# Turning the normalised rows of a four-layer graph network by transposing transfers instead of TensorE

## The chip, the cores and the metric

The kernel runs on one core of a Trainium2 chip. A core has TensorE (PE, matrix products into PSUM), VectorE (DVE), ScalarE (ACT), GpSimd (POOL), SyncE (SP, which only issues transfers here) and 16 DMA engines that the issuing queues share. Each engine takes its instructions strictly in order and waits on semaphores. The metric is the time of one execution in device microseconds.

## The reference

`x` is 8 x 2048 x 128 in float32, `adj` a symmetric 2048 x 2048 adjacency. Four layers follow each other, each adding its result to `x`; each begins with the same normalisation:

```python
h = jnp.maximum(_layernorm(x, axis=-1), 0.0)
```

Layers 0, 1 and 3 are graph attention with rank-one scores; layer 0 in full, the others differ in scaling, a residual and the `elu`:

```python
Wh = jnp.einsum('bnc,dc->bnd', x, W)
f1 = Wh @ a1
f2 = Wh @ a2
e = jax.nn.leaky_relu(f1[:, :, None] + f2[:, None, :], negative_slope=0.2)
e = jnp.where(adj[None] > 0, e, NEG_BIG)
attention = jax.nn.softmax(e, axis=-1)
h_prime = jnp.einsum('bij,bjd->bid', attention, Wh)
return jax.nn.elu(h_prime)
```

Layer 2 is attention with four heads of 32 channels, the rows against themselves:

```python
scores = jnp.einsum('bihk,bjhk->bhij', x, x)
scores = jax.nn.leaky_relu(scores, negative_slope=ALPHA)
scores = jnp.where(adj_matrix[None, None, :, :] == 0, -jnp.inf, scores)
probs = jax.nn.softmax(scores, axis=-1)
out = jnp.einsum('bhij,bjhk->bihk', probs, x)
```

## The kernel before

The order of all instructions is written by a small planner inside the kernel, when the program is built. Every step is added with `add(engine, us, due, emit, needs, takes, frees, lag)`: the engine, an assumed duration, a due time, what it emits, the steps it needs, the buffers it takes and frees. `Plan.run` (L200 on) places steps one by one: of those that an engine could start within `WINDOW_US` of the earliest, the one with the smallest due time comes first. The resulting order of each engine is emitted as it is. So the numbers in `TOKENS`, `BEATS`, `LEADS`, `EARLY` and `SHIFTS` are due times and offsets, which only set the order; they are no measured times.

A unit is one layer of one batch. There are 32 units, 31 of which are interleaved over most of the span. Each unit first prepares its rows in four quarters of 512 rows:

- `rows_made` (L528): DVE takes statistics of `x` (L470), POOL the power (L113), ACT writes a quarter of normalised rows into an `h` tile (L537, four instructions; layer 3 adds four more, L544).
- `transposes` (L563): PE turns the quarter's four 128 x 128 blocks into a PSUM bank pair (L568).
- `Gat.beginning` (L574), layers 0, 1 and 3: ACT copies the turned quarter to `h_t` in SBUF (L589; DVE in batch 0, layer 0), PE projects it (L598), ACT takes exponentials and scales the rows into `y`.
- `Heads.beginning` (L940), layer 2: SP stores the rows to DRAM (`values`, L951); ACT writes the turned quarter, rounded, to `hi` (L963), DVE the remainder to `lo` (L967), SP stores both to DRAM (`halves`, L972), from where `s`, `m` and `v` are read back for each head (L986, L994, L999).

Then the main work follows. A token of layers 0, 1 and 3 is one DVE instruction (`front`, L766, 128 x 1024 into `zg`) and eight f32 products on PE (L775, two matmul records each). There are 768 tokens. A beat of layer 2 is two pairs of score products on PE (L1061), two exps on ACT (L1068), a mask with a sum on DVE (L1074) and the weighing products on PE (L1083). There are 512 beats; two are weighed together, in batch 7 one alone (`SINGLY`).

PSUM has eight banks. Two pairs (`pair`) serve scores, transposes, projections and the small turns alike; the rest hold sums. In SBUF there are three `h` tiles, two `h_t`, one `hi` and one `lo`, five `z`, three `zg`.

The transposes are emitted by

```python
for k in range(4):
    nc.tensor.transpose(pk[:, k, :], self.h[q][:, k, :], ident)
```

Of the kernel before, what the change touches and what calls it, by code (L numbers as in the profile page):

```python
# [8 lines left out]
F32 = mybir.dt.float32  # L9
# [3 lines left out]
U8 = mybir.dt.uint8  # L13
F8 = mybir.dt.float8e4
# [26 lines left out]
def adj_preln_d4(ctx: ExitStack, tc: tile.TileContext, x, adj, w0, a0, w1, a1, w3, a3,  # L41
# [112 lines left out]
    class Op:  # L154
# [8 lines left out]
    EARLY = dict(front=-488.9, score=652.2, exp=89.3, mask=-87.7, sums=-385.5)  # L163

    SINGLY = (7,)
# [7 lines left out]
        30: 15.0, 93: 158.9, 113: -50.7, 115: -69.2, 121: 83.4, 131: -98.9, 135: -82.4, 139: -197.1,  # L173
        143: 102.0, 147: -358.4, 151: -347.8, 1041: 215.9, 1099: -157.5, 2060: -98.7, 2063: -123.3,
        2886: -204.2, 2890: -250.3, 3168: 266.3, 3549: 134.1, 5962: 12.1, 6178: 39.8, 6183: -12.0,
    }

    class Plan:
# [4 lines left out]
        ENTER_US, LEAVE_US = 0.19, 0.13  # L183
# [16 lines left out]
        def run(self):  # L200
# [9 lines left out]
            for _ in self.ops:  # L210
# [31 lines left out]
                for name, taker in op.frees:  # L242
                    self.slots[name].append((op.end, taker if isinstance(taker, int) else taker.got[name]))
                self.order.append(op)
                for u in op.users:
                    u.left -= 1
                    u.ready = max(u.ready, op.end)
                    if not u.left:
                        ready[u.engine].append(u)

    def fast(ctx):
# [9 lines left out]
        plan = Plan(dict(pair=(4, 6), sums=(0,), more=(1,), low=0, z=5, zg=3, r=2, h=3, h_t=2, hi=1, lo=1,  # L261
# [184 lines left out]
        class Unit:  # L446
# [81 lines left out]
            def rows_made(self, part, step):  # L528
# [4 lines left out]
                def rows(op, q):  # L533
                    self.h[q] = blocks(quarter("h", bufs=3))
                    for k in range(4):
                        n = q * 4 + k
                        nc.scalar.activation(self.h[q][:, k, :], X[self.b][:, n, :], AF.Relu,  # L537
                                             scale=key["rstd"][:, n:n + 1], bias=key["nmr"][:, n:n + 1])
# [23 lines left out]

            def transposes(self, q, part, made, takes):  # L563

                def turn(op):
                    pk = ps[:, op.got["pair"], :].rearrange("p (k t) -> p k t", t=P)
                    for k in range(4):
                        nc.tensor.transpose(pk[:, k, :], self.h[q][:, k, :], ident)  # L568

                return add("PE", 0.45, self.due(part), turn, made[1:], takes=["pair"] + takes,  # L570
                           frees=[("h", made[0])])

        class Gat(Unit):
            def beginning(self):  # L574
# [6 lines left out]
                for q in range(4):  # L581
                    part = 0.2 + step * q
                    turn = self.transposes(q, part, made[q], ["h_t"])
# [3 lines left out]
                    def copy(op, q=q, turn=turn, begins=begins):  # L587
# [3 lines left out]
                    copied = add("DVE" if begins else "ACT", 0.61 if begins else 0.47, self.due(part), copy,  # L591
                                 [turn], frees=[("pair", turn)])
# [166 lines left out]
            def token(self, a, due, place, last_front, last_back, first, last, gate=None):  # L759
# [21 lines left out]
                f = add("DVE", 1.2, due - EARLY["front"], front, [last_front, r_ready, rows_in[jb], powers, gate if first else None], takes=["zg"],  # L781
# [157 lines left out]
        class Heads(Unit):  # L939
            def beginning(self):  # L940
# [13 lines left out]
                for q in range(4):  # L954
# [4 lines left out]
                    turn = self.transposes(q, part, made[q], ["hi", "lo"])  # L959

                    def high(op, q=q, turn=turn):
                        self.h_t[q, 0] = quarter("hi", F32R, 1)
                        nc.scalar.copy(self.h_t[q, 0], ps[:, turn.got["pair"], :])  # L963

                    def low(op, q=q, turn=turn):
                        self.h_t[q, 1] = quarter("lo", F32R, 1)
                        nc.vector.tensor_sub(self.h_t[q, 1], ps[:, turn.got["pair"], :],  # L967
                                             self.h_t[q, 0].bitcast(F32))
# [6 lines left out]
                    hi = add("ACT", 0.47, self.due(part), high, [turn])  # L975
                    lo = add("DVE", 0.61, self.due(part), low, [hi], frees=[("pair", turn)])
                    for k, (tag, op) in enumerate((("hi", hi), ("lo", lo))):
                        self.there.append(add("SP", 1.9, self.due(part + 0.02), lambda op, q=q, k=k: store(op, q, k),
                                              [op, kept], frees=[(tag, turn)], lag=2.5))
# [39 lines left out]
            def beats(self, heads):  # L1019
# [4 lines left out]
                for h, (start, step) in enumerate(heads):  # L1024
                    ops = self.load(h, start - 24.0)
                    for jb in range(NB):
# [3 lines left out]
                        for c2 in range(2):  # L1030
                            score = add("PE", 0.455, due - EARLY["score"] + c2, lambda op, s=s, c2=c2: self.scores(op, s, c2),
                                        [score, ops[jb // HB], ops[2]], takes=["pair"] + ["z"] * (c2 == 0))
                            if c2 == 0:
                                z_taker = score
                            exps.append(add("ACT", 1.0, due - EARLY["exp"] + c2, lambda op, s=s, c2=c2, sc=score: self.exp(
                                op, s, c2, sc.got["pair"]), [score], frees=[("pair", score)]))
# [4 lines left out]
                        mask = add("DVE", 2.3, due - EARLY["mask"], lambda op, s=s: self.mask(op, s), [mask] + exps)  # L1041
                        last.append((z_taker, mask))
                        self.masks.append(mask)
                        if jb % 2 or self.b in SINGLY:
# [3 lines left out]
                                        frees=[("z", z) for z, _ in last], tiled=True)  # L1048
# [80 lines left out]
            (1, 0, 0): (-1862.2, 4.85), (0, 1, 0): (-1216.0, 6.8), (0, 1, 1): (-220.6, 7.44),  # L1129
            (1, 0, 1): (528.7, 6.78), (2, 0, 0): (550.0, 6.16), (2, 0, 1): (-497.7, 10.12),  # L1130
            (3, 0, 0): (-82.3, 6.88), (1, 1, 0): (-1087.3, 8.75), (1, 1, 1): (-509.3, 5.83),
            (3, 0, 1): (-535.5, 4.96), (2, 1, 0): (170.9, 4.67), (2, 1, 1): (470.1, 7.94),
            (0, 3, 0): (304.0, 5.97), (0, 3, 1): (1007.2, 9.21), (3, 1, 0): (733.5, 6.81),
            (3, 1, 1): (1096.6, 5.79), (4, 0, 0): (707.7, 8.19), (4, 0, 1): (1082.3, 7.42),
            (1, 3, 0): (679.2, 7.79), (1, 3, 1): (958.8, 8.29), (4, 1, 0): (339.6, 9.68),
            (4, 1, 1): (926.2, 6.01), (5, 0, 0): (364.1, 4.11), (5, 0, 1): (713.9, 3.72),
            (2, 3, 0): (403.9, 2.85), (2, 3, 1): (779.2, 8.43), (5, 1, 0): (1329.8, 4.89),
            (5, 1, 1): (1475.1, 4.64), (6, 0, 0): (1098.2, 9.62), (6, 0, 1): (2950.0, 2.74),
            (3, 3, 0): (714.9, 6.41), (3, 3, 1): (3074.8, 6.4), (6, 1, 0): (2322.0, 7.03),
            (6, 1, 1): (4526.2, 10.07), (7, 0, 0): (2367.7, 7.52), (7, 0, 1): (2792.7, 6.45),  # L1140
            (7, 1, 0): (3548.0, 7.16), (7, 1, 1): (703.3, 8.6), (4, 3, 0): (4508.6, 7.53),
            (4, 3, 1): (5355.2, 5.92), (5, 3, 0): (4546.5, 7.89), (5, 3, 1): (5580.5, 5.75),
            (6, 3, 0): (3207.4, 5.91), (6, 3, 1): (5060.7, 8.36), (7, 3, 0): (5056.1, 5.64),
            (7, 3, 1): (6837.9, 10.03),
        }
        BEATS = {
            (0, 0): (-161.82, 3.21), (0, 1): (-919.72, 17.96), (0, 2): (-887.13, 24.2),
            (0, 3): (-199.99, 2.71), (1, 0): (-3459.48, 5.01), (1, 1): (-2558.28, 2.95),
            (1, 2): (-1489.16, 0.88), (1, 3): (-1318.69, 13.71), (2, 0): (-3871.2, 28.01),
            (2, 1): (-3418.31, 16.49), (2, 2): (-2569.33, 8.93), (2, 3): (-2119.51, 26.98),  # L1150
            (3, 0): (-1533.49, 0.19), (3, 1): (-1186.31, 15.62), (3, 2): (-748.22, 30.04),
            (3, 3): (-461.43, 41.91), (4, 0): (-305.77, 24.84), (4, 1): (-1349.31, 6.1),
            (4, 2): (13.32, 12.05), (4, 3): (19.17, 4.92), (5, 0): (-143.54, 17.7),
            (5, 1): (217.07, 37.91), (5, 2): (1547.2, 30.19), (5, 3): (2881.53, 42.93),
            (6, 0): (-65.94, 14.65), (6, 1): (985.66, 4.87), (6, 2): (1381.17, 7.9),
            (6, 3): (1254.02, 32.72), (7, 0): (-270.44, 3.58), (7, 1): (647.92, 27.69),
            (7, 2): (1457.66, 3.08), (7, 3): (2140.19, 3.89),
        }
        LEADS = {
            (0, 0): 256.75, (1, 0): 1070.77, (0, 1): 113.95, (2, 0): 1008.81, (1, 1): 1403.32,  # L1160
            (3, 0): 2680.39, (2, 1): 1534.69, (0, 3): 2009.19, (3, 1): 161.18, (4, 0): 1161.93,
            (1, 3): 732.86, (4, 1): 2419.32, (5, 0): 117.85, (2, 3): 1514.41, (5, 1): 1335.63,
            (6, 0): 823.02, (3, 3): 53.23, (6, 1): 1576.41, (7, 0): 1398.84, (4, 3): 255.55,
            (7, 1): 112.36, (5, 3): 472.39, (6, 3): 2332.33, (7, 3): 369.52, (0, 2): -172.84,
            (1, 2): 2456.2, (2, 2): 2358.43, (3, 2): -660.3, (4, 2): -1280.62, (5, 2): 1703.98,
            (6, 2): -1462.99, (7, 2): 1504.7,
# [253 lines left out]
```

## Time and profile before

| | |
|---|---|
| median of 3 runs | 2731.74 us (2730.69 to 2733.18) |
| span of the profiled execution, first to last instruction | 2729.7 us |
| L568 transposes on PE | 512 instructions, first at 10.7 us, last at 2638.8 us |
| L589 copy to `h_t` on ACT | 92, 557 to 617 ns |
| L963 `hi` on ACT, L967 `lo` on DVE | 32 each, 581 and 684 ns |
| L441 ACT over 128 x 2048 | 8, 1996 ns |
| L707 ACT copy of 128 x 1024 | 6, 1006 ns |
| L867 DVE addition of 128 x 1024 in SBUF | 6, 1219 ns |
| transfers | 196.47 MB, mean 72 GB/s |

The page gives the span of the profiled execution and no other time of its own; the median of the runs is 2.0 us above it. Busy time of an engine is the union of its instructions, and matmuls overlap, so PE's busy time includes the latency of the last of each burst. In the rows of groups the columns are line, engine, operation, tile written and read, shapes and count, then busy us, mean ns of one, and idle time of the engine just before them with what ended it. In the rows of waits: who waited for whom, us in total, times, the longest. In the rows of transfers: tiles, issuing queue, count, size of each, median us from issue to landing. In the rows of the timeline: start, us, what.

### The profile page before, as it was taken

The page shows a single profiled execution, that of the slowest core. Times are in us where ns is not written, and L with a number is a line of the kernel's source. Part 1 is how long each engine was busy: PE and PEld are TensorE (multiplying, and loading weights), DVE is VectorE, ACT ScalarE, POOL GpSimd, SP SyncE. Part 2 cuts the span into 40 slices and gives each one's busy share as a digit, 9 for nine tenths or more (in the row PEclk, how much of TensorE's full clock was granted, in tenths as well). Part 3 has the DMA queues.
Part 4 walks back from the last instruction along what each step waited for, and adds up shares of the span by engine and source line. Part 5 has one row for each costly group of instructions (what it writes and reads, how often), then busy time and mean ns, then how long its engine had stood idle before and what let it go on. Part 6 is the DMA issues. An engine that isn't in the chain of part 4 may idle for free. (4 is left out here: it accounts for less than half of the span.)

```text
span 2729.7 us, 49006 instructions
## 1 busy us (share of the span) xinstructions
PE 2621.9 (96%) x20104; PEld 2016.2 (74%) x20104; DVE 2488.5 (91%) x3304; ACT 1727.6 (63%) x2777; POOL 286.1 (10%) x143
## 2 busy tenths in 40 slices
PE   7999999999999999999999999999999899999997
PEld 6899877857766777767777777777785377666687
DVE  7767989999989999998999989999999799999987
ACT  3524465667676675666856567675655956787651
POOL 1200010111101011010101011011111101101010
PEclk9999999999999999999999999999999999999999
DMA  8003323252344233443433433424234321623211
GB/s 313 17 9 90 71 59 63 47 101 55 63 120 72 60 84 55 82 74 63 87 77 56 93 58 77 87 50 79 48 76 88 63 39 37 127 55 70 36 40 41
DMA packets 216873, 196.47 MB, mean 72 GB/s; under 512 B 142896, under 2 KB 178176, under 8 KB 210496
## 3 DMA queue, kind: packets, MB, share of 16 engines
q1 hardware_dynamic: 144112, 156.46, 22.3%
q0 software_dynamic: 72112, 36.73, 11.6%
q8 instruction: 160, 2.62, 0.4%
q14 instruction: 73, 0.60, 0.1%
q10 hardware_dynamic: 416, 0.07, 0.0%
HBM read 123.03 MB, written 33.73 MB: 57 GB/s over the span
## 5 line engine op out<-in xcount | busy, mean ns | idle before, releaser
L1068 ACT ACTIVATE z<-ps,shift 128x1024 f32<-128x1024 f32 x1024 | 1122.2, 1114 | 699.9 <-PE ps L1061 697.4
L775 PEld LDWEIGHTS ps<-y,zg 128*128 128x128 f32 x12288 | 1460.8, 192 | 74.3 <-DVE zg L766 25.4
L775 PE MATMUL ps<-y,zg 128*128 128x129 f32 x12288 | 1493.4, 276 | 16.7 <-DVE zg L766 11.9
L1074 DVE SCALAR_TENSOR_TENSOR z<-z,edge 128x2048 f32<-128x2048 f32 x512 | 1169.3, 2285 | 73.6 <-ACT z L1068 71.1
L766 DVE SCALAR_TENSOR_TENSOR zg<-r,cr,edge 128x1024 f32<-128x1024 f32 x768 | 969.0, 1277 | 92.9 <-PE ps L775 84.0
L1061 PE MATMUL ps<-m,s 128*128 128x512 f32 x2048 | 717.3, 436 | 47.3 <-ACT z L1068 44.1
L1061 PEld LDWEIGHTS ps<-m,s 128*128 128x128 f32 x2048 | 313.7, 190 | 321.9 <-ACT z L1068 222.5
L1083 PE MATMUL ps<-z,v 128*32 128x512 f32 x4096 | 502.6, 602 | 2.4 <-DVE z L1074 2.2
L1083 PEld LDWEIGHTS ps<-z,v 128*32 128x32 f32 x4096 | 103.9, 109 | 237.4 <-issue 190.5
L537 ACT ACTIVATE h<-x,nmrx,rstdx 128x128 f32<-128x128 f32 x512 | 210.6, 492 | 37.0 <-DVE nmrx L118 30.0
L113 POOL TENSOR_TENSOR rstdx<-varx,neg_half 128x16 f32<-128x16 f32 x31 | 130.1, 4196 | 568.5 <-DVE varx L108 559.4
L844 POOL DMA_DIRECT2D x<-oa x40 | 35.9, 897 | 918.0 <-DVE oa L808 269.3
L1108 POOL DMA_DIRECT2D x<-o x31 | 66.1, 2133 | 510.6 <-DVE o L1103 500.0
L598 PEld LDWEIGHTS ps<-rhs,h_t 128*128 128x128 f32 x768 | 99.3, 195 | 15.5 <-DVE h_t L589 5.1
L598 PE MATMUL ps<-rhs,h_t 128*128 128x130 f32 x768 | 104.8, 281 | 5.3 <-DVE h_t L589 4.2
L470 DVE BATCH_NORM_STATS2 st<-x 128x6 f32<-128x128 f32 x496 | 105.9, 278 | 0.7 <-DMA x<-oa 0.7
L568 PE MATMUL ps<-ident,h 128*128 128x128 f32 x512 | 80.2, 278 | 4.4 <-ACT z L1068 2.8
L568 PEld LDWEIGHTS ps<-ident,h 128*128 128x128 f32 x512 | 62.6, 142 | 21.6 <-ACT z L1068 6.1
L808 DVE TENSOR_TENSOR oa<-ps,rs 128x384 f32<-128x384 f32 x144 | 73.9, 513 | 5.0
L589 ACT COPY h_t<-ps 128x512 f32<-128x512 f32 x92 | 53.3, 582 | 37.2 <-PE ps L568 37.2
L636 ACT ACTIVATE y<-ps,y 128x128 f32<-128x128 f32 x240 | 68.4, 369 | 0.0
L814 ACT ACTIVATE oe<-oa 128x1024 f32<-128x1024 f32 x32 | 33.9, 1060 | 54.2 <-DVE oa L833 51.3
(129 smaller groups left out, 835.0 us busy)
## 6 DMA issues: line engine op xcount, KB each, us to landing
s<-halves SPq DMA_DIRECT2D x256, 128.0 KB, 2.8
m<-halves SPq DMA_DIRECT2D x64, 512.0 KB, 6.9
r<-row SPq DMA_DIRECT2D x42, 512.0 KB, 3.8
x<-oa POOLq DMA_DIRECT2D x40, 512.0 KB, 5.0
raw<-in_adj_dram SPq DMA_DIRECT2D x16, 1024.0 KB, 16.2
values<-h SPq DMA_DIRECT2D x32, 256.0 KB, 2.4
halves<-hi SPq DMA_DIRECT2D x128, 64.0 KB, 1.7
halves<-lo SPq DMA_DIRECT2D x128, 64.0 KB, 1.7
```

Of the source, the lines that this page charges most:

```text
L113: nc.gpsimd.tensor_tensor(out=rstd, in0=v, in1=neg_half, op=OP.pow)
L470: nc.vector.bn_stats(out=key["st"][:, n, :], in_=rows()[:, n, :])
L537: nc.scalar.activation(self.h[q][:, k, :], X[self.b][:, n, :], AF.Relu, scale=key["rstd"][:, n:n + 1], bias=key["nmr"][:, n:n + 1])
L568: nc.tensor.transpose(pk[:, k, :], self.h[q][:, k, :], ident)
L598: nc.tensor.matmul(pv[:, k, :C + 2], lhsT=self.h_t[q][:, k * P:(k + 1) * P], rhs=rhs, start=True, stop=True)
L766: nc.vector.scalar_tensor_tensor(z, self.r[half], self.cr[:, 0, jb:jb + 1], edge[:, jb, half * HN:(half + 1) * HN], op0=OP.max, op1=OP.mult)
L775: nc.tensor.matmul(ps[:, self.banks(half, place)[i // 3], k * CE:(k + 1) * CE], lhsT=z[:, i * P:(i + 1) * P], rhs=self.y[:, jb, :], start= ...
L808: nc.vector.tensor_mul(key["a"][:, i0:i1, :], pv[:, :, :C], r[:, i0:i1, None].to_broadcast([P, i1 - i0, C]))
L1061: nc.tensor.matmul(ps[:, lo + c, :], lhsT=self.S[h, jb // HB][:, at:at + P], rhs=self.M[h][:, (c2 * 2 + c) * 512:(c2 * 2 + c + 1) * 512], ...
L1068: nc.scalar.activation(self.z[s][:, c2 * HN:(c2 + 1) * HN], ps[:, lo:lo + 2, :].rearrange("p b t -> p (b t)"), AF.Exp, bias=shift)
L1074: nc.vector.scalar_tensor_tensor(self.z[s], self.z[s], 1.0, edge[:, jb, :], op0=OP.mult, op1=OP.mult, accum_out=self.den[:, h, jb:jb + 1])
L1083: nc.tensor.matmul(ps[c * HD:(c + 1) * HD, 0, :], lhsT=self.V[h][:, jb, :], rhs=z[:, c * 512:(c + 1) * 512], start=jb == 0, stop=jb == NB - 1,
```

## The change

In all units but batch 0, layer 0, the quarter is no longer turned by PE. `turned_by_transfer` puts three steps in its place. `split`, on ACT, copies the 512 float32 of each partition as 1024 16-bit integers into `pl`, the lower halves in one plane and the upper ones in the other. `move`, on SP, issues one transfer that transposes `pl` in 128 x 128 blocks of 16-bit elements into `tr`. `merge`, on ACT, writes the two turned planes interleaved into `h_t`, which has float32 again. Layers 0, 1 and 3 project from that `h_t`. In layer 2 ACT writes `hi` from it, DVE subtracts `hi` in place, and the transfers that store `lo` read `h_t`. In layer 2 `move` also needs the transfer that stores `values`, and the `h` tile is freed by the move; elsewhere by the split. There are two `h` tiles instead of three, one `pl`, one `tr` and no `lo`.

The planner's assumed durations are altered in several places, an operation's lag no longer counts toward a user on the same engine, and a beat's `z` may be freed before the whole weighing ends. All due times are new: `SHIFTS` are zero, `TOKENS` stand on a grid of 56 us with 3.5 us between tokens, `BEATS`, `LEADS` and `EARLY` have other values.

```diff
-    EARLY = dict(front=-488.9, score=652.2, exp=89.3, mask=-87.7, sums=-385.5)
+    EARLY = dict(front=-8.1, score=-8.25, exp=367.65, mask=-66.36, sums=-45.79)
+    PLANES, TURNED, ON_PE = 1, 1, ((0, 0),)
+    SPLIT_US, MOVE_US, MOVE_LAG_US, MERGE_US = 1.0, 1.2, 3.0, 1.0
...
-        ENTER_US, LEAVE_US = 0.19, 0.13
+        ENTER_US, LEAVE_US = 0.09, 0.21
...
-                    u.ready = max(u.ready, op.end)
+                    u.ready = max(u.ready, op.end - (op.lag if u.engine == op.engine else 0.0))
...
-        plan = Plan(dict(pair=(4, 6), sums=(0,), more=(1,), low=0, z=5, zg=3, r=2, h=3, h_t=2, hi=1, lo=1,
+        plan = Plan(dict(pair=(4, 6), sums=(0,), more=(1,), low=0, z=5, zg=3, r=2, h=2, h_t=2, pl=1, tr=1, hi=1,
...
+            def turned_by_transfer(self, q, part, made, kept=None):
+                key = {}
+                def split(op):
+                    key["pl"] = big.tile([P, 2, 4 * P], U16, tag="pl", name="pl", bufs=PLANES)
+                    nc.scalar.copy(key["pl"], self.h[q].rearrange("p k c -> p (k c)").bitcast(U16).rearrange(
+                        "p (n two) -> p two n", two=2))
+                def move(op):
+                    key["tr"] = big.tile([P, 8, P], U16, tag="tr", name="tr", bufs=TURNED)
+                    nc.sync.dma_start_transpose(out=key["tr"], in_=key["pl"].rearrange("p two n -> p (two n)"))
+                def merge(op):
+                    self.h_t[q] = quarter("h_t")
+                    nc.scalar.copy(self.h_t[q].bitcast(U16).rearrange("p (n two) -> p two n", two=2),
+                                   key["tr"].rearrange("p (two k) n -> p two (k n)", two=2))
+                parted = add("ACT", SPLIT_US, self.due(part), split, made[1:], takes=["pl"], frees=[] if kept else [("h", made[0])])
+                moved = add("SP", MOVE_US, self.due(part), move, [parted, kept], takes=["tr"],
+                            frees=[("pl", parted)] + [("h", made[0])] * (kept is not None),
+                            lag=MOVE_LAG_US)
+                return add("ACT", MERGE_US, self.due(part), merge, [moved], takes=["h_t"], frees=[("tr", moved)])
...
-                    turn = self.transposes(q, part, made[q], ["h_t"])
+                    by_pe = (self.b, layer) in ON_PE
+                    turn = self.transposes(q, part, made[q], ["h_t"]) if by_pe else None
...
+                    else:
+                        copied = turn = self.turned_by_transfer(q, part, made[q])
...
-                    turn = self.transposes(q, part, made[q], ["hi", "lo"])
+                    turn = self.turned_by_transfer(q, part, made[q], kept)
...
-                        nc.scalar.copy(self.h_t[q, 0], ps[:, turn.got["pair"], :])
+                        nc.scalar.copy(self.h_t[q, 0], self.h_t[q])
...
-                        nc.vector.tensor_sub(self.h_t[q, 1], ps[:, turn.got["pair"], :],
-                                             self.h_t[q, 0].bitcast(F32))
+                        self.h_t[q, 1] = self.h_t[q].bitcast(F32R)
+                        nc.vector.tensor_sub(self.h_t[q, 1], self.h_t[q], self.h_t[q, 0].bitcast(F32))
...
-            (1, 0, 0): (-1862.2, 4.85), (0, 1, 0): (-1216.0, 6.8), (0, 1, 1): (-220.6, 7.44),
+            (1, 0, 0): (92.0, 3.5), (0, 1, 0): (148.0, 3.5), (0, 1, 1): (204.0, 3.5), (1, 0, 1): (260.0, 3.5),
...
-            (0, 0): (-161.82, 3.21), (0, 1): (-919.72, 17.96), (0, 2): (-887.13, 24.2),
+            (0, 0): (304.8, 9.3), (0, 1): (453.55, 4.32), (0, 2): (522.61, 0.05), (0, 3): (510.06, 6.98),
...
-            (0, 0): 256.75, (1, 0): 1070.77, (0, 1): 113.95, (2, 0): 1008.81, (1, 1): 1403.32,
+            (0, 0): -228.72, (1, 0): 333.0, (0, 1): 2800.2, (2, 0): 323.39, (1, 1): 2219.45, (3, 0): 175.69,
```

## The prediction

> **What bounds the kernel now.** I read part 1 of the page first, then the busy time by stretch of the span, the groups of instructions, the waits, the timeline of single stretches and the transfers.
>
> ```profile
> PE 2621.9 (96%) x20104; PEld 2016.2 (74%) x20104; DVE 2488.5 (91%) x3304; ACT 1727.6 (63%) x2777; POOL 286.1 (10%) x143
> ```
>
> ```profile
> core 0: us, PE busy (x) PEld busy (x) DVE busy (x) ACT busy (x) POOL busy (x), PEclk, DMA share, GB/s
> 300.00:2700.00 2400.00, 2332.87 (x17646) 1742.03 (x17643) 2239.94 (x2882) 1598.75 (x2424) 249.37 (x116) 1.00 0.35 68
> 0.00:300.00 300.00, 274.07 (x2331) 259.41 (x2331) 231.97 (x406) 126.71 (x351) 36.74 (x27) 0.98 0.35 109
> ```
>
> Two engines are nearly full at once: from 300 to 2700 us PE is busy 97% and DVE 93%. ACT has a third of its time free. The granted clock is full, so no gain hides there.
>
> ```profile
> L1068 ACT ACTIVATE z<-ps,shift 128x1024 f32<-128x1024 f32 x1024 | 1122.2, 1114 | 699.9 <-PE ps L1061 697.4
> L775 PE MATMUL ps<-y,zg 128*128 128x129 f32 x12288 | 1493.4, 276 | 16.7 <-DVE zg L766 11.9
> L1074 DVE SCALAR_TENSOR_TENSOR z<-z,edge 128x2048 f32<-128x2048 f32 x512 | 1169.3, 2285 | 73.6 <-ACT z L1068 71.1
> L766 DVE SCALAR_TENSOR_TENSOR zg<-r,cr,edge 128x1024 f32<-128x1024 f32 x768 | 969.0, 1277 | 92.9 <-PE ps L775 84.0
> L568 PE MATMUL ps<-ident,h 128*128 128x128 f32 x512 | 80.2, 278 | 4.4 <-ACT z L1068 2.8
> L589 ACT COPY h_t<-ps 128x512 f32<-128x512 f32 x92 | 53.3, 582 | 37.2 <-PE ps L568 37.2
> ```
>
> A PE matmul here lasts 276 ns, but the next one starts long before that, so PE's price must be read from start to start:
>
> ```profile
> 760.68 0.60 PE L568 MATMUL ps<-ident,h 128*128 128x128 f32 x4
> 761.12 1.95 PE L775 MATMUL ps<-y,zg 128*128 128x129 f32 x16
> 762.83 0.71 PE L1061 MATMUL ps<-m,s 128*128 128x512 f32 x2
> ```
>
> The four transposes of a quarter hold PE for 0.44 us (760.68 to 761.12), a token 1.70 us; in the same way a pair of score products takes 0.54 and a beat's weighing 0.93. By such prices PE has 768 tokens, 1024 score pairs, 512 weighings and some 180 us of the rest: 2522 us, 92% of the span and hardly above DVE's 2488. PE alone doesn't bound the kernel; the two do together.
>
> ```profile
> ACT z L1068 <- PE ps L1061: 697.4, 625, 4.0
> DVE z L1074 <- ACT z L1068: 71.1, 109, 2.8
> PE ps L1061 <- ACT z L1068: 44.1, 86, 1.4
> ACT h_t L589 <- PE ps L568: 37.2, 12, 29.5
> ACT hi L963 <- PE ps L568: 22.8, 14, 7.0
> ```
>
> ACT mostly waits for PE. The last two rows are 60.0 us in which ACT stood still for the transposes that are now taken from PE.
>
> **The change part by part.**
>
> Removed from PE: the built order of the changed kernel keeps 16 of the 512 transposes, those of batch 0, layer 0, so 124 quarters go. 124 x 0.436 (the median; 0.44 above) = 54.1 us. The transposes also held one of the two PSUM pairs that scores use; PE's waits for ACT are 44 us in all, the bound of a gain there, and I count none of it. In DVE's 2488 us nothing goes: the 32 low halves now read SBUF instead of PSUM, 0.68 us each, and by half of an addition of 1024 SBUF elements (1219 ns) 0.61: 2 us, nil.
>
> The order laid out anew: I cut both built orders into stretches of 100 us of PE work and set beside each the DVE work that must be done by its end. Of one late stretch: the new order has 24 tokens and 28 beats, DVE 24 x 1.22 + 28 x 2.22 + 16 for statistics and endings = 107 us; the old one has 31 and 21 there, and 99 us. The new order puts beats later (376 of 512 by token 608, before 402), and a beat costs DVE more than PE. What DVE has beyond PE, summed over the stretches, is 39 us in the old order and 70 in the new: +32. So PE's gain is in good part lost to DVE.
>
> ACT: 92 copies of 0.58 go (-53), 124 splits and 124 joins of 1024 16-bit elements come. No row has a 16-bit copy. Bounds: 0.58 if a pair passes as one 4-byte element, 2.0 if an element two or four bytes apart costs double (L441 takes 1996 ns for 2048). I take 1.0, L707's 1006 ns for 1024 elements. 248 - 53 = +195, ACT at some 1922 us, 71%. It is hidden under the 697 us in which ACT waits for PE, except in one stretch near 2200 us, where ACT has 113 us of work beside DVE's 107: +6.
>
> The transfers: 124 on SP's queue, 0.25 MB each, 31 MB beside the page's 196 MB. From split to join ACT now waits for a landing that the trace does not show. The rows of 256 KB:
>
> ```profile
> values<-h SPq DMA_DIRECT2D x32, 256.0 KB, 2.4
> v<-values SPq DMA_DIRECT2D x32, 256.0 KB, 5.0
> x<-o POOLq DMA_DIRECT2D x31, 256.0 KB, 7.8
> ```
>
> 2.4 has pieces of 512 bytes, 5.0 pieces of 128 bytes, 7.8 pieces of 128 bytes with an addition. In the code every row of tr gathers 16-bit elements from 128 partitions, so pieces are not longer than values' 512 bytes, and v's 5.0 is nearest; 2.4 and 7.8 stay as ends. The planner's own figure, 1.2 + 3.0, is an assumption of the code and no evidence.
>
> Queued behind the waiting join are the exps, for which PE's scores wait (two PSUM pairs), and the projections of the quarter, which in PE's new order mostly stand 0 to 2 score pairs after it. What covers the landing is the ACT work between split and join: the median is 5.0 us of busy time, at 71% 7.0 us of elapsed time. For instance four rows and two exps: 4 x 0.41 + 2 x 1.10 = 3.8, elapsed 5.4. Summed over 120 quarters (the first four have nothing between), what is missing to a landing L is 11 us at L = 2.4, 32 at 4.2, 45 at 5.0, 77 at 6.0, 170 at 7.8 and 376 at 10. Against it stand the 60 us of waits for PE that go. At 5.0 the two nearly cancel; I take 0.
>
> The Trainium skill, "VectorE: DVE Perf Modes", "The three transpose paths", speaks against the change: it lists 1309 ns for a 128x128 two-byte block by DMA and 390 by TensorE, and advises TensorE where PSUM will do. Eight such blocks in a row would be 10.5 us, some 430 us missing and a time near 3085, an estimate from that page. "Advanced Engine Details and Errata", "X-Bar Transpose (TRN2)", says that such transfers are as fast as ordinary ones: then 2.4 holds, and 2678 at best. No row here decides between the pages.
>
> SP: an issue holds its queue 0.38 us by values' row; 47 us in all, under waits for scores of 950 us. But 24 of the 124 moves stand right behind loads of s or v that wait for PE (up to 38.4 us in one case before), and 16 s loads stand right behind a move, so a late split delays a load. Planned waits, priced nothing; if the cover goes, each costs what it is late. One pl and one tr tile make a unit serial: 1.0 + 5.0 + 1.0 a quarter, 28 us a unit, 868 us for 31 units; it fits in 2700. Rows held in two h tiles instead of three free up at the split or the landing: nothing while L is under the 7 us above.
>
> Sum against the span: 2729.7 - 54.1 + 32 + 6 + 0 = 2713.6. The median of the runs is 2.0 above the span: **2715.5**.
>
> **Rivals.**
> - Full gain: PE sets the end throughout, and the waits between the engines shrink with it. For it: PE's 97%. Against: DVE's 93% and the later beats. 2731.7 - 54 = 2678.
> - No change: DVE keeps its 2488 us and its 241 us of idle time, and what PE saves becomes waiting. For it: DVE zg <- PE is only 84 us in all. 2731.
> - Late transfers, slower: joins stand in ACT's queue before exps and projections. From L = 6 on (77 - 60 = 17, the whole remaining gain) the kernel is slower. At 7.8 it is 170 - 60 = 110, half to all of which reaches the end, since PE and DVE have no room to catch up: 2770 to 2825. For it: x<-o's 7.8 and the ninth tenth of v at 9.4. Against: values' 2.4.
> - Slower by ACT: 2.0 us per split and join puts ACT at 2170 us; the stretches after 2200, at 95 to 113 of 107, gain some 10 to 14 each, and projections come late: about 2745.
> - That the change does less than it says is excluded by the built order: 124 transfers, 16 transposes left.
>
> **How the numbers follow.** My forecast, 2690 to 2726, 0.33; full gain 0.10; no change 0.10; late transfers 0.34; ACT 0.13. So faster 0.43, slower 0.47, same 0.10, where 0.2% is 5.5 us, about what a measurement of this kernel tells from no change. The signs are nearly even, but the single likeliest price of a landing is 5.0, hence 2715. The range goes from full gain, 2680, to the late transfers at 7.8 counted whole, 2825; outside are half of the full gain (0.05) and landings above 8 us (0.12).
>
> **What would show it.** PE's transposes x16 with 2 to 3 us busy; split and join near 1.0 us; tr's landing (5.0; 6 is the turning point); ACT's idle time before the join, 45 to 55 us in total; DVE's share at 92% or more with PE's falling to about 94%. Wrong would be: a landing above 6, joins waiting over 100 us, ACT above 75%, or a DVE share that stays at 91% with a shorter span's gain of 50.

## The result and the profile after

The changed kernel takes 2682.98 us (median of 4, 2681.98 to 2683.54), the kernel before 2731.22 in the same series: a ratio of 0.9822, interval 0.9808 to 0.9836, 48 us faster. The prediction was 2715.5, with 2680 as its lower end; its rival "full gain" said 2678.

Part 1 of the page after, then the busy time of two stretches:

```profile
PE 2570.5 (96%) x19608; PEld 2003.5 (75%) x19608; DVE 2483.1 (93%) x3304; ACT 1929.7 (72%) x2933; POOL 277.5 (10%) x143
```

```profile
300.00:2650.00 2350.00, 2284.22 (x17187) 1727.72 (x17187) 2230.88 (x2879) 1776.95 (x2574) 242.09 (x115) 0.99 0.43 82
0.00:300.00 300.00, 269.27 (x2273) 259.05 (x2274) 232.24 (x405) 148.20 (x349) 35.37 (x28) 0.97 0.42 118
```

PE's busy time fell by 51 us, near the 54 us of the transposes that left it. It is a union of overlapping matmuls, though, and part of it ran at half clock (below), so this is no exact check. DVE has the same work as before, 2483 against 2488 us, so nearly the whole gain can be read as DVE's idle time: 2729.7 - 2488.5 = 241 us before, 2681.8 - 2483.1 = 199 us now. From 300 us on DVE is busy 95% instead of 93. ACT has 202 us more work.

The clock changed too. The mean granted TensorE clock of the profiled run is 0.985, before it was 0.994. The trace gives full clock or half, so that is 80 us at half clock instead of 34. PE was busy in 60 and in 22 of these. At half clock the products of a token start 214 ns apart in the median, otherwise 112, so the work takes about twice as long. That is some 19 us of lost PE time in the changed kernel, (60 - 22) / 2, an estimate; how much of it reaches the end is not shown. The gain came in spite of it.

The groups of the page, with the two new ACT steps:

```profile
L1102 ACT ACTIVATE z<-ps,shift 128x1024 f32<-128x1024 f32 x1024 | 1094.2, 1114 | 395.3 <-PE ps L1095 384.7
L1108 DVE SCALAR_TENSOR_TENSOR z<-z,edge 128x2048 f32<-128x2048 f32 x512 | 1162.3, 2285 | 46.7 <-ACT z L1102 46.4
L798 DVE SCALAR_TENSOR_TENSOR zg<-r,cr,edge 128x1024 f32<-128x1024 f32 x768 | 967.3, 1279 | 82.3 <-PE ps L807 74.6
L582 ACT COPY h_t<-tr 128x1024 uint16<-128x1024 uint16 x124 | 168.2, 1357 | 48.9 <-DMA tr<-pl 45.4
L573 ACT COPY pl<-h 128x1024 uint16<-128x1024 uint16 x124 | 130.0, 1049 | 0.9
```

DVE's masks wait 46 us for exps instead of 71, its fronts 75 for PE instead of 84: of DVE's 42 us these two are 34. ACT now waits 385 us for PE's scores instead of 697. Where ACT stood for PE's transposes (60 us), it stands 45 us for the transfers.

Three groups of 256 KB transfers and the transposing ones of the same run (us to landing last; the trace gives the transposing ones no size):

```profile
values<-h SPq DMA_DIRECT2D x32, 256.0 KB, 2.4
v<-values SPq DMA_DIRECT2D x32, 256.0 KB, 3.7
x<-o POOLq DMA_DIRECT2D x31, 256.0 KB, 7.8
tr<-pl SPq DMA_TRANSPOSE x124, 3.1
```

One quarter in the timeline, ACT and then SP:

```profile
837.94 1.04 ACT L573 COPY pl<-h 128x1024 uint16<-128x1024 uint16 x1
838.87 3.20 ACT L541 ACTIVATE h<-x,nmrx,rstdx 128x128 f32<-128x128 f32 x8
842.19 2.12 ACT L1102 ACTIVATE z<-ps,shift 128x1024 f32<-128x1024 f32 x2
844.20 1.35 ACT L582 COPY h_t<-tr 128x1024 uint16<-128x1024 uint16 x1
```

```profile
839.00 1.28 SPq L578 DMA_TRANSPOSE tr<-pl x1
```

The split ends at 838.98, the transfer is issued at once, lands at 842.07 by its semaphore, and the join comes at 844.20, after eight rows and two exps that ACT had to do anyway. This is the usual case: from the end of a split to the landing the median is 3.27 us, three quarters are under 5.0, nine tenths under 7.1, the longest 51. Of the 31 above 5.0, 21 were issued a microsecond or more after the split had ended; in the others the landing itself took 5 to 7 us. In ACT's order the join starts 5.4 us after the split in the median.

### The profile page after: what moved, and what is told of

Its sections match the earlier page's. It is cut to its first block, busy times and chain, and to the rows that moved or that the text cites. A ratio compares the mean times of both kernels' runs of the same rounds, so it can differ in the third digit from the quotient of the medians.

```text
span 2681.8 us, 48498 instructions
## 1 busy us (share of the span) xinstructions
PE 2570.5 (96%) x19608; PEld 2003.5 (75%) x19608; DVE 2483.1 (93%) x3304; ACT 1929.7 (72%) x2933; POOL 277.5 (10%) x143
## 5 line engine op out<-in xcount | busy, mean ns | idle before, releaser
L807 PE MATMUL ps<-y,zg 128*128 128x129 f32 x12288 | 1476.3, 277 | 22.1 <-DVE zg L798 21.7
L1102 ACT ACTIVATE z<-ps,shift 128x1024 f32<-128x1024 f32 x1024 | 1094.2, 1114 | 395.3 <-PE ps L1095 384.7
L1095 PE MATMUL ps<-m,s 128*128 128x512 f32 x2048 | 642.8, 426 | 32.7 <-ACT z L1102 30.0
L1095 PEld LDWEIGHTS ps<-m,s 128*128 128x128 f32 x2048 | 338.6, 190 | 282.7 <-ACT z L1102 151.4
L582 ACT COPY h_t<-tr 128x1024 uint16<-128x1024 uint16 x124 | 168.2, 1357 | 48.9 <-DMA tr<-pl 45.4
L114 POOL TENSOR_TENSOR rstdx<-varx,neg_half 128x16 f32<-128x16 f32 x31 | 117.8, 3799 | 600.0 <-DVE varx L109 583.8
L573 ACT COPY pl<-h 128x1024 uint16<-128x1024 uint16 x124 | 130.0, 1049 | 0.9
L708 ACT ACTIVATE y<-y,f 128x128 f32<-128x128 f32 x128 | 51.8, 484 | 3.6 <-DVE f L698 3.6
```

The costliest lines, as they stand in the source:

```text
L114: nc.gpsimd.tensor_tensor(out=rstd, in0=v, in1=neg_half, op=OP.pow)
L573: nc.scalar.copy(key["pl"], self.h[q].rearrange("p k c -> p (k c)").bitcast(U16).rearrange("p (n two) -> p two n", two=2))
L582: nc.scalar.copy(self.h_t[q].bitcast(U16).rearrange("p (n two) -> p two n", two=2), key["tr"].rearrange("p (two k) n -> p two (k n)", two=2))
L807: nc.tensor.matmul(ps[:, self.banks(half, place)[i // 3], k * CE:(k + 1) * CE], lhsT=z[:, i * P:(i + 1) * P], rhs=self.y[:, jb, :], start= ...
L1095: nc.tensor.matmul(ps[:, lo + c, :], lhsT=self.S[h, jb // HB][:, at:at + P], rhs=self.M[h][:, (c2 * 2 + c) * 512:(c2 * 2 + c + 1) * 512], ...
L1102: nc.scalar.activation(self.z[s][:, c2 * HN:(c2 + 1) * HN], ps[:, lo:lo + 2, :].rearrange("p b t -> p (b t)"), AF.Exp, bias=shift)
```

## The experiments

Two kinds are told apart. In the first the order of all engines is that of the kernel it is made from, and only what a step does is changed. In the second the planner lays the order out anew, by the same due times unless it is said otherwise. The kernel before ran in each series, with medians of 2730.8 to 2732.0; the changed kernel's 2683.0 is from the first series alone.

### The order untouched: what is a microsecond of each engine worth?

Less PE work in the old order (`e3_old_order_one_turn`) and under the new due times (`e15_new_due_times_one_turn`, made from the second kind's first run below). Of each quarter's four transposes one is done, and its block is copied four times, so three blocks of four hold wrong values:

```diff
-                    for k in range(4):
+                    for k in range(4 if (self.b, self.layer) == (0, 0) else 1):
                         nc.tensor.transpose(pk[:, k, :], self.h[q][:, k, :], ident)
...
+                            nc.scalar.copy(blocks(self.h_t[q]), ps[:, turn.got["pair"], None, :P].to_broadcast([P, 4, P]))
```

> The kernel before, its order untouched, but of each quarter's four transposes only the first is done (not in batch 0, layer 0) and copied four times, so three blocks of every four rows-blocks are wrong values. PE loses 124 x 0.327 = 40.5 us of work and nothing else changes. Theory A, PE sets the end: 2731 - 40 = 2691 (2688 to 2700). Theory B, what the prediction used, DVE takes over for a good part: 2708 or more.

> The kernel with the new due times and PE turning (2738), order untouched, with one transpose of four per quarter done and copied four times (three blocks of four hold wrong values), so 40.5 us less PE work. Theory shared, as in the old order: 0.5 to 0.7 of it, 2710 to 2718. Theory PE alone: 2695 to 2702.

Measured: 2707.3 (ratio 0.9916, 0.9899 to 0.9932), 24 us of 40.5, just below the bound of the theory that DVE takes over for a good part; and 2734.9 against 2738.0, 3 us of 40.5. Neither theory had foreseen that: in that second order the removed PE work hardly shows.

The clock is part of why. In the old order it is no lower with the one transpose than with four (0.994 to 0.996 against 0.992 to 0.995). In the second order it is: 0.977 to 0.979 against 0.984 to 0.989. Two stretches of the second run, the rows of busy time with the clock third from the end, and then eight projections in each (start, us):

```profile
2088.00:2096.00 8.00, 4.97 (x36) 2.69 (x35) 4.16 (x5) 8.00 (x22) 0.00 (x0) 1.00 0.61 117
2097.00:2114.00 17.00, 13.53 (x42) 8.04 (x46) 5.36 (x6) 15.07 (x38) 2.15 (x1) 0.51 0.45 43
```

```profile
2091.66 1.16 PE L633 MATMUL ps<-rhs,h_t 128*128 128x130 f32 x8
2098.01 2.10 PE L633 MATMUL ps<-rhs,h_t 128*128 128x130 f32 x8 [0.52 <-ACT h_t L621]
```

In the profiled runs PE was busy at half clock for 86 us here and for 43 with all four transposes, which is 21 us of the missing 37, by an estimate that halves the difference. The other runs with four transposes had a lower clock than the profiled one (0.985 against 0.989), and by theirs it is nearer 14. What swallowed the rest is open.

More PE work, in both kernels (`e4_more_pe_after`, `e4b_more_pe_before`):

```diff
                     def project(op, q=q):
                         lo = op.got["pair"]
+                        for k in range(4):
+                            nc.tensor.transpose(ps[:, lo, k * P:(k + 1) * P], self.h_t[q][:, k * P:(k + 1) * P], ident)
```

> The changed kernel, order untouched, with four more transposes on PE ahead of each projection, into banks that the projection then overwrites: 96 x 0.436 = 42 us more PE work. Theory A: 2683 + 42 = 2725 (2717 to 2727). Theory B, DVE at 93% already sets the end: 2702 or less.

> The kernel before with the same four more transposes ahead of each projection, 42 us more PE work, order untouched. Theory A: 2731 + 42 = 2773 (2765 to 2775). Theory B: 2752 or less.

Measured: 2708.5 and 2763.1, that is 25.5 and 31.7 us of 42. In both kernels it lies between the two theories: PE is a bound, but not the only one.

More DVE work (`e5_more_dve_after`, `e6_more_dve_before`):

```diff
-                    for n in range(q * 4, q * 4 + 4):
+                    for n in [*range(q * 4, q * 4 + 4), q * 4, q * 4 + 2]:
                         nc.vector.bn_stats(out=key["st"][:, n, :], in_=rows()[:, n, :])
```

> The changed kernel, order untouched, with half as many statistics again: 312 more instructions of 0.197 us, 61 us more DVE work. Theory shared (PE and DVE set the end in turn, as the added PE work suggests, of which 61% showed): 0.4 to 0.6 of it, 2708 to 2720. Theory PE alone: under 2693. Theory DVE alone: 2735 or more.

> The kernel before with the same 61 us more DVE work, order untouched. Of PE's added work 75% showed there. Theory shared: 0.25 to 0.45 of it, 2746 to 2759, and less than in the changed kernel. Theory PE alone: under 2741.

Measured: 2739.2 (+56 of 61) and 2780.0 (+48 of 61), both above what the theory of a shared bound gave. DVE's busy time rose by 59 and 58 us. A microsecond of DVE costs 0.9 in the changed kernel and 0.8 before, one of PE 0.6 and 0.75. After the change DVE's work is the dearer, as the forecast had it. Part of that price is PE's clock: with the added DVE work PE was busy at half clock for 81 us instead of 60, half of which is 10 of the 56 us, and with the added PE work for 52. Before, these are 27 and 20 us against 22. With the clock's part taken off, 46 of 61 are left in both kernels, so it is not shown that DVE itself became the harder bound.

More ACT work (`e7_split_twice`) and a later landing (`e8_moved_twice`):

```diff
                 def split(op):
...
+                    for _ in range(2):
+                        nc.scalar.copy(key["pl"], self.h[q].rearrange("p k c -> p (k c)").bitcast(U16).rearrange(
+                            "p (n two) -> p two n", two=2))
```

```diff
                 def move(op):
...
+                    for _ in range(2):
+                        nc.sync.dma_start_transpose(out=key["tr"], in_=key["pl"].rearrange("p two n -> p (two n)"))
```

> The changed kernel with every split done twice: 124 x 1.05 = 130 us more ACT work, and each transfer 1.05 us later. ACT would be at 2060 us. Theory of the prediction, ACT's work is hidden under its waits for PE but for a few stretches: 2690 to 2703. Theory coupled, ACT in its strict order delays scores and projections: 2710 to 2750.

> The changed kernel with every transposing transfer issued twice, the second after the first has landed: the landing goes from 3.1 to some 6.2 us. The prediction's table of missing cover has about 18 us at 3.1 and 85 at 6.2, so ACT waits some 65 us more: 2715 to 2750 if half to all of that reaches the end. Theory slack, the order's own reserve of about 1 us and ACT's free time hide it: under 2700.

Measured: 2764.3 (+81 for 130 us of ACT work) and 2960.8 (+278). Both theories of little cost fall, and both times are beyond what either theory gave. The waits of the run with the doubled transfer:

```profile
ACT z L1103 <- PE ps L1096: 383.5, 296, 11.6
ACT h_t L583 <- DMA tr<-pl: 317.1, 100, 15.5
DVE zg L799 <- PE ps L808: 159.0, 158, 7.1
```

Joins wait 317 us instead of 45, 272 more, and the kernel takes 278 us longer, nearly one for one. ACT is idle for 752 us in the changed kernel, but its wait for PE's scores is as long with the doubled transfer as without (384 and 385 us): it did not shrink to make room for the late joins. PE and DVE came late in turn: fronts wait 159 us for PE instead of 75, and PE was busy at half clock for 183 us instead of 60, so some 61 of the 278 us may be PE's clock, by the same estimate. How the 278 divide is not shown.

### The order laid out anew

PE turning under the new due times (`e2_new_due_times_pe`):

```diff
-    PLANES, TURNED, ON_PE = 1, 1, ((0, 0),)
+    PLANES, TURNED, ON_PE = 1, 1, tuple((b, k) for b in range(8) for k in range(4))
...
-                    turn = self.turned_by_transfer(q, part, made[q], kept)
+                    turn = self.transposes(q, part, made[q], ["hi", "h_t"])
```

> The changed kernel's planner constants and due times, but all quarters are turned by TensorE again (one low tile is an h_t). Theory A, PE's 54 us are the whole gain and the new order by itself brings nothing: 2683 + 54 = 2737 (2725 to 2748). Theory B, the new order brings much of the gain and the transposes little: under 2715.

Measured: 2738.0 (1.0026, 1.0015 to 1.0038), 1 us from what theory A said. Taken alone it would show that the transposes are the whole gain. The run with one transpose of four in this very order (3 us for 40) shows that it does not: in this order most of what PE gives is lost elsewhere. The due times were made for the other steps, and this kernel keeps two `h` tiles instead of the old three and uses an `h_t` tile for `lo`; which of these costs what wasn't tried.

So the next runs tell the planner of a longer step, or change nothing but a planner's figure. The doubled transfer and the doubled split, planned for (`e9_moved_twice_planned`, `e10_split_twice_planned`), and a PSUM pair held by each join (`e11_pair_held`); the doubled copy and transfer themselves are those shown above:

```diff
-    SPLIT_US, MOVE_US, MOVE_LAG_US, MERGE_US = 1.0, 1.2, 3.0, 1.0
+    SPLIT_US, MOVE_US, MOVE_LAG_US, MERGE_US = 1.0, 4.3, 2.6, 1.0
```

```diff
-    SPLIT_US, MOVE_US, MOVE_LAG_US, MERGE_US = 1.0, 1.2, 3.0, 1.0
+    SPLIT_US, MOVE_US, MOVE_LAG_US, MERGE_US = 2.0, 1.2, 3.0, 1.0
```

```diff
-                return add("ACT", MERGE_US, self.due(part), merge, [moved], takes=["h_t"], frees=[("tr", moved)])
+                merged = add("ACT", MERGE_US, self.due(part), merge, [moved], takes=["h_t", "pair"], frees=[("tr", moved)])
+                merged.frees.append(("pair", merged))
+                return merged
```

> As the run with every transfer issued twice, which took 2961, but the planner is told of it: 4.3 us of SP's queue and 2.6 us to the landing in place of 1.2 and 3.0, so the order is laid out anew by the same due times. Theory plan (what a step costs is decided by whether the order was laid out for it): 2690 to 2750. Theory length (a landing of 6 us costs this much in any order): 2900 or more.

> As the run with every split done twice, which took 2764, but the planner is told of a split of 2.0 us. Theory plan: 2683 to 2715. Theory work (130 us more on ACT cost this in any order): 2750 to 2780.

> The changed kernel, but the planner lets each join hold a PSUM pair, as the copy of a turned quarter did; nothing else is done with it, and the order is laid out anew. Theory pairs (the PSUM pairs that the transposes no longer take give the part of the gain that PE's work doesn't): 2700 to 2715. Theory none: 2675 to 2695.

Measured: 2881.2, 2793.6 and 2783.7. Planning for the later landing wins back 80 of 278 us, between the theories. Planning for the longer split costs 29 us more than not planning for it, against both. The held pair costs 101 us, far more than its theory gave, so it can't be told from the loss by a new laying out, and how much the freed PSUM pairs bring stays open.

Neutral changes: only a figure of the planner is altered, no instruction is added or taken away.

```diff
-    SPLIT_US, MOVE_US, MOVE_LAG_US, MERGE_US = 1.0, 1.2, 3.0, 1.0
+    SPLIT_US, MOVE_US, MOVE_LAG_US, MERGE_US = 1.0, 1.2, 3.0, 1.3
```

```diff
-                f = add("DVE", 1.195, due - EARLY["front"], front,
+                f = add("DVE", 1.2, due - EARLY["front"], front,
```

> The changed kernel; the planner's figure for a join is 1.3 us in place of 1.0 (the trace has 1.36) and the order is laid out anew by the same due times; no instruction is added or removed. Theory searched order (the due times fit one order, and any new laying out loses): 2700 to 2790. Theory insensitive: 2675 to 2692.

> The changed kernel; the planner's figure for a token's front is 1.200 in place of 1.195, nothing else; the order is laid out anew. Theory searched order: 2700 to 2790, as far off as with the join's figure. Theory insensitive: 2675 to 2692.

> The kernel before; the planner's figure for a token's front is 1.195 in place of 1.2, nothing else. Theory searched order: 2745 to 2830. Theory insensitive: 2722 to 2740.

> The kernel before; the planner's figure for a mask is 2.29 in place of 2.3, nothing else. Theory searched order: 2745 to 2830. Theory insensitive: 2722 to 2740.

> The changed kernel; the planner's figure for a mask is 2.23 in place of 2.22, nothing else: a third neutral laying out anew of the same steps, after 2724 and 2672. Theory searched order: 2690 to 2740, since two of three other such changes lost 37 and 41. Theory insensitive: 2672 to 2692.

| kernel | figure altered | us | against its own kernel |
|---|---|---|---|
| changed | none | 2683.0 | |
| changed | join 1.3 | 2723.7 | +41 |
| changed | front 1.2 | 2671.8 | -11 |
| changed | mask 2.23 | 2680.8 | -2 |
| before | none | 2732.0 | |
| before | front 1.195 | 2737.5 | +6 |
| before | mask 2.29 | 2769.0 | +37 |

Against the expectations, the join's figure and the mask's in the kernel before fall under a searched order, the front's before and the mask's in the changed kernel under an insensitive one, and the front's in the changed kernel is faster than either said.

So the same steps take from 2672 to 2724 us in the changed kernel and from 2731 to 2769 before, by order alone. Compared place by place in the traces, PE's instructions agree with the changed kernel's in 95% of places with the front's figure, in 69% with the join's. The two ranges are 7 us apart, and their medians (2682 and 2738) 56. Of the runs this is the best evidence for what the change as a whole, with its altered planner, is worth apart from one order's luck. It is four and three orders, no more.

Page rows of the best and the worst of the changed kernel's neutral orders:

```profile
PE 2567.1 (96%) x19608; PEld 1998.4 (75%) x19608; DVE 2482.0 (93%) x3304; ACT 1929.7 (72%) x2933; POOL 278.0 (10%) x143
```

```profile
PE 2587.4 (95%) x19608; PEld 2006.5 (74%) x19608; DVE 2484.6 (91%) x3304; ACT 1930.6 (71%) x2933; POOL 270.6 (10%) x143
```

DVE's and ACT's work agree to 3 us. Spans of 2670.5 and 2721.5 make DVE's idle time 188 and 237 us: there the difference lies. The slower one has the lower clock, 0.978 against 0.986, and PE was busy at half clock for 87 us against 52; half of that difference is 17 of the 52 us between them, an estimate.

Last, figures nearer to the traces, and due times searched anew for them (`s1_searched`; the tables of due times are left out, and so are the front's figure, now 1.2, and two constants of the planner that were searched too):

```diff
-    SPLIT_US, MOVE_US, MOVE_LAG_US, MERGE_US = 1.0, 1.2, 3.0, 1.0
+    SPLIT_US, MOVE_US, MOVE_LAG_US, MERGE_US = 1.02, 1.24, 3.0, 1.3
...
-    EARLY = dict(front=-8.1, score=-8.25, exp=367.65, mask=-66.36, sums=-45.79)
+    EARLY = dict(front=-8.04, score=-8.37, exp=378.81, mask=-66.85, sums=-47.01)
```

> The changed kernel's steps; the planner is told of what the traces show (split 1.02, transfer 1.24 and 3.0, join 1.3, front 1.2) and its due times are searched anew for these figures. Told of such a join by the old due times it took 2724. Theory searched order: the loss is won back and more, 2655 to 2685. Theory that the figures themselves cost: 2705 or more.

Measured: 2682.7 (0.9832, 0.9810 to 0.9855). The 41 us that the truer figure of the join had cost are won back, but nothing beyond the changed kernel. Not by due times alone: the front's 1.2, which by itself was worth 11 us, is in it. The fastest version of all is the changed kernel with the front's figure at 1.2: 2671.8, ratio to before 0.9781 (0.9765 to 0.9797). It is the best of several orders, so a part of its lead is selection.

## Why the prediction was right and wrong

- **What bounds the kernel: right.** PE and DVE both bind: added work of either lengthens the kernel (0.6 a microsecond of PE, 0.9 of DVE after the change), and neither price is 1. PE's share did not fall to 94% as forecast; it stayed at 96%.
- **Transposes, 124 x 0.436 = 54.1 us off PE: right as work taken away.** How much of it shows depends on the order. In the old order 0.6 does, so the transposes by themselves are some 32 us there (0.6 x 54; 24 of 40.5 were measured).
- **"So PE's gain is in good part lost to DVE", +32, and +6 for ACT: here it failed.** The term was the order's, worked out from the work in stretches of 100 us, with the rest of the span, 169 us, taken as it was. Two ways of measuring it agree that it was far too high. Under the new due times with PE turning, the kernel is 7 us slower than before, where the term said 32; from there the transfers bring 55 us, about the whole 54. By the fixed-order price instead, the transposes bring 32 of the 48 us, and -16 is left for the order and for all that ACT and the transfers cost, where I had +38. The two divide the 48 us differently, and neither is the changed kernel's own order with PE turning.

  The new order does put beats late: in the traces DVE has done 370 masks by its 608th front, before 385. But DVE's idle time is not fixed by such sums. Orders with the same work differ by 52 us, and in the changed one DVE waits 25 us less for exps and 9 less for PE. A sum over 100 us can't see a wait of 1 to 8 us. That the new order as such is better than the old one is not shown, since they order different steps.
- **The clock, put at nothing: it counts.** "The granted clock is full" was a reading of the kernel before. Some 19 us more of PE's time were lost to half clock in the changed kernel, and the order decides how much it is.
- **Split and join at 1.0 us: too low, and the sum right by luck.** The split takes 1.05, the join 1.36, together 298 us instead of 248. ACT is at 1930 us all the same, where 1922 were forecast: its busy time is a union, and its instructions overlap their neighbours more than before (exps 1094 us instead of 1122 at the same 1114 ns each). "It is hidden under the 697 us" was wrong as a rule: 130 us more in a fixed order cost 81. That it holds for this work because the new order was made around it is likely, not shown; telling the planner of a longer split did not win the loss back.
- **The landing, 5.0: too long.** 3.1 us, nearer to values' 2.4. I chose by the size of the pieces; v's own 5.0 is 3.7 in the run after, so a part of it was the moment and not the pieces. ACT's wait for transfers was forecast at 45 to 55 us and is 45; with the shorter landing my table gives about 18, so this agrees by two errors.
- **Late transfers, turning point at 6: the mechanism right, the price far too low.** Twice the transfer gave a median of 7.1 us from split to landing and 317 us of waits; the table has some 130 there. The step that fails is the division of ACT's work between split and join by its busy share, 0.71. Without it, with ACT's work between split and join as the traces have it, the sum is some 280. So ACT's idle time lies mostly elsewhere than between a late split and its join.
- **Full gain, 2678, held at 0.10, is what came out to 5 us,** but not for its reason: PE doesn't set the end throughout, as added PE work shows only to 0.6 and added DVE work shows too. The near match is luck as far as the runs tell.

What stays open: how the 48 us divide between PE's relief, the PSUM pairs, PE's clock and the fit of one order. The old due times with the transfers weren't tried.

## What to carry to other kernels

Where two engines are both over 90% busy, price a removed microsecond by an experiment in a fixed order (repeat or drop some of that engine's work) instead of by shares: here it was 0.6 for PE and 0.9 for DVE. Do it in the order that you will keep: in another one 40 us of PE work were worth 3. Compare the granted clock of the two runs as well. An order searched for one exact set of steps is a term of its own, of up to 40 us here; before a change is judged by one new order, lay both versions out a few times by neutral changes and compare the ranges. A transfer put between two steps of an engine needs work of that engine between them that covers the landing by itself; counting on the engine's idle time gave here less than half of the waits that came.

## What the runs showed of the hardware

- The granted TensorE clock of a single core depends on the order: 0.954 to 0.996 over these kernels and runs. At half clock eight projections took 2.10 us instead of 1.16, and a token's products started 214 ns apart instead of 112.
- A transposing transfer of 128 x 1024 16-bit elements holds SP's queue for 1.24 us (values' rows 0.38) and lands 3.1 us after its issue begins, 8.1 at most; 124 of them add 130,945 packets and 32.5 MB, about 250 bytes each.
- ACT reads 16-bit elements four bytes apart in 1.05 us for 1024, and writes them so in 1.36.
- In one queue the second of two such transfers to the same tile, issued after the first has landed, takes again 3.1 us in the median.
